# A click-model kernel on one Trainium2 core: the dense head after the history loop, laid out anew

## The chip, the core and the metric

The kernel runs on one core of a Trainium2 chip. That core has a matrix engine (TensorE, PE in the profile), VectorE (DVE), ScalarE (ACT), GpSimd (POOL) and SyncE (SP), each with an instruction queue of its own that runs in order; they meet through semaphores. On-chip data lies in SBUF (128 rows, or partitions) and in PSUM, into which PE writes its sums. DMA queues move data to and from the device's memory. The metric is the device time of one execution in microseconds (us).

## What is computed

The reference is a recommendation model with attention over a user's history. There are B = 16384 samples, each with L = 200 items of history; every table row has D = 64 numbers. Everything is float32.

```python
def dice(x, alpha, axis):
    mean, var = mean and variance of x along axis
    p = sigmoid((x - mean) * rsqrt(var + EPS))
    return x * (p + alpha * (1.0 - p))
u, it, c = u_emb[user], i_emb[item], c_emb[cate]      # B x 64 each
h = i_emb[hist]                                       # L x B x 64
feat = concatenate([h, it, h - it, h * it])           # L x B x 256
a = dice(feat @ au_W1 + au_b1, au_alpha, axis=1)      # L x B x 36
w = a @ au_W2 + au_b2                                 # L x B x 1
cur = sum(w * h, axis=0)                              # B x 64
z = concatenate([u, it, c, cur])                      # B x 256
z = dice(z @ W1 + b1, alpha1, axis=0)                 # B x 80
z = dice(z @ W2 + b2, alpha2, axis=0)                 # B x 40
return z @ W3 + b3                                    # B x 2
```

Two things matter for the order of the work. A dice needs the mean and the variance over the whole batch, so that each of its layers has to be finished before the next can start. And of the four inputs of the head's first layer only `cur` needs the loop over the history: `u`, `it` and `c` are there from the beginning.

## The kernel before

**Tiling.** The 16384 samples are 128 partitions by NT = 128 row tiles. Eight chunks (ND = 8) of TD = 16 row tiles each cover the batch; a chunk is 2048 samples. Transposed, with the 64 numbers of a row along the partitions, a chunk has CD = 1024 columns, with samples of one half of the row tiles on one half of the partitions (this is the `g` of the code: two groups of samples share 128 partitions). A step of the main loop is one chunk of one history position, so there are 200 x 8 = 1600 steps.

**Prologue (L194-270).** The item table is copied to device memory as `table`, each row followed by its product with a part of the first attention weight, so that one gather brings both. `fetch_one` and `keep_one` gather the rows of item, user and category (384 gathers, L138), transpose them and keep the item's in `itT`, and put the others into device memory as `ucT`. `xi`, the item's share of the attention layer, goes there too.

**Main loop.** `For_i` at L411 runs 8 times over 24 history positions each (192 steps); the last 8 positions (64 steps) are straight-line code (L415), with ten more steps that only drain. The order within a step is written out by hand, in `step` (L376), and is kept on each engine:

- `fetch(k)`: 16 indirect DMAs on POOL (L138) bring 128 rows each into one of 12 `land` buffers; SP loads `xit` (L309).
- ACT: a sigmoid into `gate` (L386) and a scaling into the PSUM buffer `pg` (L389), for step k-10.
- ACT: copy `xit` into PSUM buffer `px` (L391), two buffers taken in turn.
- `turn(k-1)`: four transposes on DVE from `land` into `hx` (L317); ACT copies the result to PSUM, `ph` (L393).
- `hidden(k-2)`: DVE adds (L329) and takes statistics (L331).
- `product(k-1)`: DVE multiplies into `hm` (L323), PE adds `hm` times a weight onto `px` (L176).
- After every eighth step, `moments` (L357-374) turns the statistics into the factors of dice, for one history position.
- `weigh(k-10)`: DVE forms the weight of each row from `pg` through `yT` and adds the weighted rows onto `cur` (L337 to L353).

A gather may write a `land` buffer only when `weigh` has done with it. Before the first step, ten `land` buffers and both `hx` are zeroed on DVE (L286, L288).

**Head (L418-507).** It stands behind the loop. Its weights are loaded there by SP (L429 to L444). Layer 1 takes each chunk c and each group g by itself: four inputs (user from `ucT`, item from `itT`, category from `ucT`, `cur` transposed by four DVE transposes) times `w1[g]`, whose rows for the other group are zero, into 80 partitions of `px[g]`. `keep` (L455) copies them with the bias to SBUF as `z` (ACT, L457) and takes statistics (DVE, L459). `col_moments` (L472) forms the factors of dice; `dice` (L477) is a sigmoid on ACT (L480) and a tensor_scalar on DVE (L481), with a product at L487; layer 2 goes from 80 to 40 partitions, again 16 times. Then dice again (product at L500), and layer 3: 256 matmuls of two columns each (L503), which give the result with samples along the partitions, an addition of the bias (L504), and one DMA (L507).

Of the kernel before, what the change touches and what calls it, by code (L numbers as in the profile page):

```python
# [14 lines left out]
P = 128  # L15
# [13 lines left out]
def din_kernel(  # L29
# [53 lines left out]
    blk_h = const.tile([P, P], F32, name="blk_h")  # L83
    blk_i = const.tile([P, P], F32, name="blk_i")
    blk_m = const.tile([P, P], F32, name="blk_m")
    au_w = const.tile([P, 4, A], F32, name="au_w")
# [39 lines left out]
    px = [psum.tile([P, CD], F32, name=f"px{i}") for i in range(2)]  # L126
# [6 lines left out]
    ucT = dram.tile([2, ND, P, CD], F32, name="ucT")  # L133

# [59 lines left out]
    with ExitStack() as start:  # L194
        pre = start.enter_context(tc.tile_pool(name="pre", bufs=3))
        ids = [start.enter_context(tc.tile_pool(name=f"ids{i}", bufs=1)).tile(
            [P, NT], I32, name=f"ids{i}") for i in range(3)]
        for t, v in zip(ids, (r_item, r_user, r_cate)):
            load_ids(t, v)
        load_hist_ids(0, 0)  # L200

        per = V // P
        rest = V - P * per
        grid = i_emb[: P * per].rearrange("(p n) d -> p n d", n=per)
        grid_out = table[: P * per].rearrange("(p n) d -> p n d", n=per)
        blocks = [(n0, min(TD, per - n0)) for n0 in range(0, per, TD)]
        if blocks[-1][1] == TD and rest:
            blocks.append((per, 0))
        tabs = {}

        def table_rows(b):

            n0, n = blocks[b]
            tab = pre.tile([P, TD, 2 * D], F32, tag="tab", name="tab")
            m = n
            if n:
                nc.sync.dma_start(tab[:, :n, :D], grid[:, n0 : n0 + n])
            if b == len(blocks) - 1 and rest:
                nc.vector.memset(tab[:, n, :D], 0.0)
                nc.sync.dma_start(tab[:rest, n, :D], i_emb[P * per :])  # L220
                m = n + 1
            rT = pre.tile([P, CD], F32, tag="rT", name="rT")
            transpose(rT, tab, m)
            layer(px[b % 2], [(blk_h, rT)], n=m * S)
            tabs[b] = tab, m

        def table_store(b):
            n0, n = blocks[b]
            tab, m = tabs.pop(b)
            transpose_back(tab[:, :, D:], px[b % 2], m)  # L230
            if n:
                nc.scalar.dma_start(grid_out[:, n0 : n0 + n], tab[:, :n])
            if m > n:
                nc.scalar.dma_start(table[P * per :], tab[:rest, n])

        def fetch_one(j):
            c, k = j % ND, j // ND
            gather(land[j % EARLY][:, :, :D], ids[k][:, ts(c, TD)], (i_emb, u_emb, c_emb)[k])

        def keep_one(j):  # L240
            c, k = j % ND, j // ND
            if k == 0:
                transpose(itT[:, c], land[j % EARLY])
                layer(ph, [(blk_i, itT[:, c])])
                t = pre.tile([P, CD], F32, tag="t", name="t")
                nc.scalar.activation(t, ph, AF.Identity, bias=au_bias)
                nc.scalar.dma_start(xi[c], t)
            else:
                t = pre.tile([P, CD], F32, tag="t", name="t")
                transpose(t, land[j % EARLY])  # L250
                nc.scalar.dma_start(ucT[k - 1, c], t)

        with tc.manual_schedule():
            done = 0
            for j in range(3 * ND + 1):
                if j < 3 * ND:
                    fetch_one(j)
                while done < len(blocks) + 1 and done < 2 * j + 2 + j // 12:
                    if done < len(blocks):
                        table_rows(done)  # L260
                    if done:
                        table_store(done - 1)
                    done += 1
                if j:
                    keep_one(j - 1)
            while done < len(blocks) + 1:
                if done < len(blocks):
                    table_rows(done)
                table_store(done - 1)
                done += 1  # L270

    with ExitStack() as main:
# [7 lines left out]
        hm = ring.tile([P, CD], F32, name="hm")  # L280
        gate = ring.tile([P, CD], F32, name="gate")
        yT = ring.tile([P, CD], F32, name="yT")
# [7 lines left out]
        for t in px:  # L290
            layer(t, [(blk_m, hx[0][:, 0])])
# [29 lines left out]
        def product(k):  # L321

            nc.vector.tensor_mul(hm, ph, itT[:, k % ND])  # L323
            layer(px[k % 2], [(blk_m, hm)], onto=True)

        def hidden(k):

            l, c = divmod(k, ND)
            nc.vector.tensor_add(x_of(k), by_row(px[k % 2]), by_row(hx[k % 2][:, 1]))  # L329
            for i in range(2):  # L330
                nc.vector.bn_stats(  # L331
                    stats[l % 2][:, 2 * c + i, :], x_of(k)[:, ts(i, TD // 2)]
                )

        def weigh(k):

            nc.vector.tensor_mul(by_row(pg), by_row(pg), x_of(k))  # L337
            nc.vector.transpose(yT, pg)  # L338
# [37 lines left out]
        def step(k, last=None):  # L376
# [7 lines left out]
            if has(k - 10):  # L384
                i = (k - 10) // ND % 2
                nc.scalar.activation(  # L386
                    by_row(gate), x_of(k - 10), AF.Sigmoid, bias=shifts[i], scale=rstds[i]
                )
                nc.scalar.activation(pg, gate, AF.Identity, bias=au_al, scale=au_1al)  # L389
            if has(k - 1):  # L390
                nc.scalar.copy(px[(k - 1) % 2], xit[(k - 1) % XI])  # L391
                turn(k - 1)
                nc.scalar.copy(ph, hx[(k - 1) % 2][:, 0])  # L393
            if has(k - 2):
                hidden(k - 2)
            if has(k - 1):
                product(k - 1)
# [5 lines left out]
        def steps(l0, n, last):  # L403

            for k in range(n * ND + (10 if last else 0)):
                l, c = divmod(k, ND)
                if c == 0 and l + 1 < n + (not last):
                    load_hist_ids((l + 1) % IDX, l0 + l + 1)
                step(k, last=n * ND - 1 if last else None)

        with tc.For_i(0, L - L % LPB, LPB) as l0:  # L411
            with tc.manual_schedule():
                steps(l0, LPB, False)
        with tc.manual_schedule():
            steps(L - L % LPB, L % LPB, True)  # L415


    with ExitStack() as head:  # L418
        fin = head.enter_context(tc.tile_pool(name="fin", bufs=1))
        work = head.enter_context(tc.tile_pool(name="work2", bufs=2))  # L420


        w1 = []
        for g in range(2):
            t = fin.tile([P, 4, Z1], F32, name=f"w1{g}")
            nc.vector.memset(t, 0.0)
            for e in range(2):
                rows = W1.rearrange("(f d) z -> d f z", d=D)[e * S : (e + 1) * S]
                nc.sync.dma_start(t[quarter(e, g)], rows)  # L429
            w1.append(t)  # L430
        w2 = fin.tile([Z1, Z2], F32, name="w2")
        nc.sync.dma_start(w2, W2)
        w3 = fin.tile([Z2, ZO], F32, name="w3")
        nc.sync.dma_start(w3, W3)
        bias1 = fin.tile([Z1, 1], F32, name="bias1")
        nc.sync.dma_start(bias1, col(b1))
        bias2 = fin.tile([Z2, 1], F32, name="bias2")
        nc.sync.dma_start(bias2, col(b2))
        bias3 = fin.tile([P, ZO], F32, name="bias3")
        nc.sync.dma_start(bias3, b3.partition_broadcast(P))  # L440
        al, al1 = [], []
        for i, (v, n) in enumerate(((alpha1, Z1), (alpha2, Z2))):
            t = fin.tile([n, 1], F32, name=f"al{i}")
            nc.sync.dma_start(t, col(v))  # L444
            u = fin.tile([n, 1], F32, name=f"al1{i}")
            nc.vector.tensor_scalar(u, t, -1.0, 1.0, ALU.mult, ALU.add)
            al.append(t)
            al1.append(u)

        z = fin.tile([Z1, 2 * ND, CD], F32, name="z")  # L450
        zstats = [
            fin.tile([n, 4 * ND, nc.vector.BN_STATS_DIM], F32, name=f"stats{i}")
            for i, n in enumerate((Z1, Z2))
        ]
        def keep(i, n, m, pz, bias):  # L455

            nc.scalar.activation(z[:n, m, :], pz[:n], AF.Identity, bias=bias)  # L457
            for j in range(2):
                nc.vector.bn_stats(zstats[i][:, 2 * m + j, :], z[:n, m, ts(j, CH)])  # L459

        for c in range(ND):
            rows = land[c % EARLY].rearrange("p (s n) d -> p s (n d)", s=2)
            for i in range(2):
                nc.sync.dma_start(rows[:, i], ucT[i, c])
# [73 lines left out]
```

## Time and profile before

| | us |
|---|---|
| median of 3 runs (32900.82 to 32961.82) | 32900.87 |
| the profiled execution | 32903.59 |
| its span in the trace | 32901.7 |
| busy in the span: DVE | 25564.2 |
| busy in the span: POOL | 24520.4 |
| busy in the span: ACT | 7641.4 |
| busy in the span: PE | 6388.8 |

The span is what lies between the first and the last instruction that the trace shows; 1.9 us of the execution lie outside it. The mean clock that TensorE was granted is 0.546 of full speed. Of the busy time, 0.944 us is one gather's time on POOL; the DMA that it starts goes on by itself. The share of busy time is a mean over the whole kernel, and nearly all of the span is the main loop; a stage of some tens of us cannot be read from it and has to be read from the timeline and from busy times over a stretch.

How the rows are read: a row of a group gives line, engine, operation, the tile written and the tiles read, shapes and a count; then busy us and the mean ns of one, then the idle us of that engine just before such instructions, with what ended most of it ("issue": nothing that the trace shows). A row of the timeline gives start, duration, engine and instruction, and in brackets the idle time before it. "x2" in a row of the PE counts passes: a float32 matmul is recorded as two. `128*80` in such a row is the stationary operand, 128 rows by 80 columns.

### The profile page before, as it was taken

To read this page: it belongs to the slowest core of one execution; us is meant where nothing else is said; L and a number is where in the kernel's file an instruction comes from. 1 tells how busy PE (TensorE), PEld (TensorE's weight loads), DVE (VectorE), ACT (ScalarE), POOL (GpSimd) and SP (SyncE) were. 2 spreads that over 40 slices of the span, in tenths; PEclk is the share of its full clock that TensorE was granted. 3 is DMA by queue.
4 is the path that set the end of the run, shared out by engine and by line. 5 is a ranking of instruction groups with operands and counts; after the bars stand their busy time and mean duration, and the time that the engine had idled before them with its cause. 6 is when DMAs were issued, how large, how long until landed. Compare 5 with 4: busy or idle time off the path is not lost. (4 is left out here: it accounts for less than half of the span.)

```text
span 32901.7 us, 99907 instructions
## 1 busy us (share of the span) xinstructions
PE 6388.8 (19%) x7216; PEld 2043.0 (6%) x7216; DVE 25564.2 (78%) x28837; ACT 7641.4 (23%) x7113; POOL 24520.4 (75%) x25988
## 2 busy tenths in 40 slices
PE   3111111111111111111111111111111111111113
PEld 0000000000000000000000000000000000000001
DVE  7777777777777777777777777777777777777776
ACT  1222222222222222222222222222222222222222
POOL 7777777777777777777777777777777777777774
PEclk6555555555555555555555555555555555555555
DMA  5222222222222222222222222222222222222221
GB/s 158 79 79 79 79 79 79 79 80 78 80 79 79 79 78 80 79 79 80 78 79 79 80 79 79 80 79 79 79 79 80 79 80 78 79 80 79 80 79 53
DMA packets 1208006, 2648.96 MB, mean 81 GB/s; under 512 B 549078, under 2 KB 575222, under 8 KB 1201142
## 3 DMA queue, kind: packets, MB, share of 16 engines
q0 software_dynamic: 831488, 1691.97, 19.8%
q1 hardware_dynamic: 365238, 887.18, 8.5%
q10 hardware_dynamic: 10560, 63.79, 0.5%
q14 instruction: 705, 5.78, 0.1%
q8 instruction: 15, 0.25, 0.0%
HBM read 2577.24 MB, written 63.91 MB: 80 GB/s over the span
## 5 line engine op out<-in xcount | busy, mean ns | idle before, releaser
L138 POOL DMA_INDIRECT land<-table,idx x25600 | 24157.7, 944 | 7880.7 <-issue 7560.7
L317 DVE STREAM_TRANSPOSE hx<-land 64x1024 f32<-64x1024 f32 x6404 | 7935.6, 1239 | 6418.2 <-DMA land<-table,idx 6265.7
L176 PE MATMUL px<-hm,blk_m 128*128 128x512 f32 x6404 | 5973.2, 1088 | 26045.0 <-DVE hm L323 26045.0
L389 ACT ACTIVATE pg<-gate,au_al,au_1al 128x1024 f32<-128x1024 f32 x1610 | 1943.8, 1207 | 12855.1 <-DVE cur L353 12854.8
L393 ACT COPY ph<-hx 128x1024 f32<-128x1024 f32 x1601 | 1627.7, 1017 | 10702.8 <-DVE hx L317 10702.8
L176 PEld LDWEIGHTS px<-hm,blk_m 128*128 128x128 f32 x6404 | 1878.9, 324 | 30138.6 <-DVE hm L323 28484.2
L331 DVE BATCH_NORM_STATS2 st<-land 128x6 f32<-128x512 f32 x3204 | 2060.6, 685 | 55.0
L338 DVE STREAM_TRANSPOSE yT<-pg 128x1024 f32<-128x1024 f32 x1610 | 2011.6, 1249 | 55.2
L352 DVE TENSOR_TENSOR pg<-land,ph 128x1024 f32<-128x1024 f32 x1610 | 1978.6, 1229 | 54.9
L353 DVE TENSOR_TENSOR cur<-pg,cur 128x1024 f32<-128x1024 f32 x1610 | 1971.2, 1224 | 55.6
L340 DVE TENSOR_REDUCE r<-yT 128x32 f32<-128x1024 f32 x1610 | 1964.0, 1220 | 55.3
L329 DVE TENSOR_TENSOR land<-px,hx 128x1024 f32<-128x1024 f32 x1602 | 1961.2, 1224 | 49.4
L386 ACT ACTIVATE gate<-land,sh,rs 128x1024 f32<-128x1024 f32 x1610 | 1991.7, 1237 | 2.9
L337 DVE TENSOR_TENSOR pg<-pg,land 128x1024 f32<-128x1024 f32 x1610 | 1967.5, 1222 | 10.7 <-ACT pg L389 10.7
L323 DVE TENSOR_TENSOR hm<-ph,itT 128x1024 f32<-128x1024 f32 x1601 | 1931.1, 1206 | 0.0
L391 ACT COPY px<-xit 128x1024 f32<-128x1024 f32 x1601 | 1591.4, 994 | 22.9 <-PE px L176 22.9
L347 DVE SCALAR_TENSOR_TENSOR ph<-r,au_bias,r 64x16 f32<-64x16 f32 x3220 | 770.7, 239 | 114.7
L386 ACT ACT_TABLE_LOAD x210 | 269.4, 1283 | 582.1 <-DMA land<-table,idx 372.3
L344 DVE COPY r<-r 64x32 f32<-64x32 f32 x1610 | 321.4, 200 | 55.0
L185 ACT ACT_TABLE_LOAD x203 | 260.4, 1283 | 3.6
L185 ACT ACTIVATE std<-var,eps 128x1 f32<-128x1 f32 x201 | 59.2, 295 | 716.5 <-DVE var L373 716.5
L176 PE MATMUL px<-rT,blk_h 128*128 128x512 f32 (+1 forms) x196 | 158.2, 942 | 231.1 <-DVE rT L159 231.1
(76 smaller groups left out, 1903.2 us busy)
## 6 DMA issues: line engine op xcount, KB each, us to landing
xit<-xi SPq DMA_DIRECT2D x1601, 512.0 KB, 3.9
land<-table,idx POOLq DMA_INDIRECT x25600, 2.5
table<-tab ACTq DMA_DIRECT2D x48, 1024.0 KB, 4.4
tab<-in_L_rec_i_emb SPq DMA_DIRECT2D x48, 512.0 KB, 4.3
idx<-in_r_hist SPq DMA_DIRECT2D x200, 64.0 KB, 1.8
ucT<-t ACTq DMA_DIRECT2D x16, 512.0 KB, 2.9
land<-ucT SPq DMA_DIRECT2D x16, 512.0 KB, 4.3
xi<-t ACTq DMA_DIRECT2D x8, 512.0 KB, 2.7
```

The source lines that it names most:

```text
L138: nc.gpsimd.indirect_dma_start(out=dst[:, n, :], out_offset=None, in_=rows, in_offset=bass.IndirectOffsetOnAxis(ap=ids[:, n : n + 1], axis=0),
L176: nc.tensor.matmul(dst[:, cols], lhsT, rhs[:, cols], start=(j == 0 and not onto), stop=(j == len(pairs) - 1), skip_group_check=onto,)
L317: nc.vector.transpose(dst.rearrange("p s (n t) -> p n s t", t=S), rows[ts(i, D), :, :, e])
L329: nc.vector.tensor_add(x_of(k), by_row(px[k % 2]), by_row(hx[k % 2][:, 1]))
L331: nc.vector.bn_stats(stats[l % 2][:, 2 * c + i, :], x_of(k)[:, ts(i, TD // 2)])
L337: nc.vector.tensor_mul(by_row(pg), by_row(pg), x_of(k))
L338: nc.vector.transpose(yT, pg)
L340: nc.vector.tensor_reduce(r, yT.rearrange("p (i n u) -> p i n u", i=2, u=S), mybir.AxisListType.X, ALU.add)
L352: nc.vector.tensor_mul(by_row(pg), rows, w.unsqueeze(2).to_broadcast([P, TD, D]))
L353: nc.vector.tensor_add(cur[:, ts(c, TD)], by_row(pg), cur[:, ts(c, TD)])
L386: nc.scalar.activation(by_row(gate), x_of(k - 10), AF.Sigmoid, bias=shifts[i], scale=rstds[i])
L389: nc.scalar.activation(pg, gate, AF.Identity, bias=au_al, scale=au_1al)
```

## The change

**Placement.** The pools `pre` and `once` are opened early and closed before the loop; the weights that only the prologue needs move to `once`. The head's tiles are allocated at the start. The two buffers `px[0]`, `px[1]` become `px`, used by every step, and `pz`. `hm` and `yT` become parts of `hx`, and `gate` becomes `pg` in place: the sigmoid and the scaling both write `pg`.

```diff
+    px, pz = (psum.tile([P, CD], F32, name=n) for n in ("px", "pz"))
...
-                    by_row(gate), x_of(k - 10), AF.Sigmoid, bias=shifts[i], scale=rstds[i]
+                    by_row(pg), x_of(k - 10), AF.Sigmoid, bias=shifts[i], scale=rstds[i]
...
-                nc.scalar.activation(pg, gate, AF.Identity, bias=au_al, scale=au_1al)
+                nc.scalar.activation(pg, pg, AF.Identity, bias=au_al, scale=au_1al)
...
-                nc.scalar.copy(px[(k - 1) % 2], xit[(k - 1) % XI])
                 turn(k - 1)
                 nc.scalar.copy(ph, hx[(k - 1) % 2][:, 0])
...
                 hidden(k - 2)
...
+                nc.scalar.copy(px, xit[(k - 1) % XI])
                 product(k - 1)
```

**Packing.** The 80 units of layer 1 are split into 64 (ZA) and 16 (ZB). The 64 of both groups of samples fill 128 partitions, one tile for each chunk. The 16 of both groups are 32 partitions, and four chunks (J = 4) share one tile of 128, each in a window of its own of a weight that is zero elsewhere. Layer 2's 40 units of both groups are 80 partitions; layer 3's two outputs of both groups and all eight chunks are 32 partitions, again by windows. A unit then has its statistics on several partitions; the mean over these is taken by a small matmul with a matrix `mean_of`, built at the very start from a unit matrix:

```diff
+    for n, t in mean_of.items():
+        m = t.shape[0] // n
+        unit = once.tile([n, m, n], F32, name=f"unit{n}")
+        nc.vector.memset(unit, 0.0)
+        nc.gpsimd.affine_select(
+            out=unit, in_=unit, compare_op=ALU.not_equal, fill=1.0, base=0,
+            pattern=[[0, m], [-1, n]], channel_multiplier=1,
+        )
+        unit = unit.rearrange("u m v -> u (m v)")
+        nc.tensor.matmul(ph[: n * m, : n * m], unit, unit, start=True, stop=True)
+        nc.vector.tensor_scalar_mul(t, ph[: n * m, : n * m], 1.0 / m)
```

In the built program the two first gathers of the prologue stand ahead of the three affine selects on POOL, and an instruction that loads GpSimd's library stands between them; it is not in the kernel before.

**Weights.** They are loaded at the end of the prologue, before the zeroing of `land`: five memsets on DVE (512, 896, 80, 320 and 60 columns), some 45 small DMAs on SP, three tensor_scalars.

```diff
+    def load_head_weights():
+        for t in (w1a, w1b, w2a, w2b, w3):
+            nc.vector.memset(t, 0.0)
+        for g in range(2):
+            for e in range(2):
+                rows = W1.rearrange("(f d) z -> d f z", d=D)[e * S : (e + 1) * S]
+                nc.sync.dma_start(w1a[quarter(e, g), :, ts(g, ZA)], rows[:, :, :ZA])
+                z0 = 2 * ZB * (J - 1) + ZB * g
+                nc.sync.dma_start(w1b[quarter(e, g), :, z0 : z0 + ZB], rows[:, :, ZA:])
...
```

**Loop.** The For_i runs 7 times; the last 32 positions (256 steps) are straight-line code. In these, `base_of_layer1` sums item, user and category for layer 1, one matmul of 512 columns behind each step (96 of them, and a step or two at each of ten evictions, in which the sum with its bias goes to device memory as `zbase`).

```diff
+                    for f, t in ((1, itT[:, c]), (0, zt[:, 0]), (2, zt[:, 1])):
+                        w = w1b[:, f, window(j)] if rest else w1a[:, f]
+                        for i in range(2):
+                            nc.tensor.matmul(
+                                pz[:, ts(i, CH)], w, t[:, ts(i, CH)],
+                                start=(f == 1 and j == 0), stop=(f == 2 and last),
+                            )
+                            yield
+                    if last:
+                        nc.scalar.activation(
+                            zt[:, 0], pz, AF.Identity, bias=(zb if rest else za)[0]
+                        )
+                        nc.sync.dma_start(zbase[ND + c // J if rest else c], zt[:, 0])
```

**Drain and head.** In the ten draining steps the fourth input is added, a chunk behind each of the last eight weighings. SP loads `zbase` into free `land` buffers, ACT copies it to PSUM, DVE transposes `cur`, and PE adds:

```diff
+            load_base(0, 1)
+            for k in range(K, K + 10):
+                step(k, last=K - 1)
+                if k < K + 4:
+                    load_base(*((2, 3), (ND, ND + 1), (4, 5), (6, 7))[k - K])
+                c = k - K - 2
+                if c >= 1:
+                    keep1(c - 1)
+                if c >= 0:
+                    layer1(c)
+            keep1(ND - 1)
...
+        def layer1(c):
+            nc.scalar.copy(px, z_of(c))
+            if c % J == 0:
+                nc.scalar.copy(pz, rest_of(c))
+            curT = xit[c % XI]
+            transpose(curT, cur[:, ts(c, TD)])
+            layer(px, [(w1a[:, 3], curT)], onto=True)
+            layer(pz, [(w1b[:, 3, window(c % J)], curT)], onto=True)
+        def keep1(c):
+            nc.scalar.copy(z_of(c), px)
+            row_sums(0, P, c, z_of(c))
+            if c % J == J - 1:
+                nc.scalar.copy(rest_of(c), pz)
+                row_sums(1, P, c // J, rest_of(c))
```

Layers 2 and 3 then go over eight chunks instead of sixteen; layer 3's matmuls all add onto one tile of 32 partitions, which is transposed once at the end:

```diff
+            fa, fb = row_factors(0, ZA, P), row_factors(1, ZB, P)
+            for c in range(ND):
+                if c % J == 0:
+                    dice(rest_of(c), rest_of(c), spare[4 + c // J], fb, zb)
+                a = spare[c % 4]
+                dice(a, z_of(c), a, fa, za)
+                po = (px, pz, pg, ph)[c % 4]
+                layer(po[: 2 * Z2], [(w2a, a), (w2b[:, c % J], rest_of(c))])
+                t = home(10 + c)[: 2 * Z2]
+                nc.scalar.activation(t, po[: 2 * Z2], AF.Identity, bias=z2[0])
+                row_sums(2, 2 * Z2, c, t)
+            f2 = row_factors(2, Z2, 2 * Z2)
+            for c in range(ND):
+                a = spare[c % 4]
+                dice(a, home(10 + c)[: 2 * Z2], a, f2, z2)
+                at = (ND - 1 - c) * 2 * ZO
+                for i in range(2):
+                    nc.tensor.matmul(
+                        px[:n, ts(i, CH)], w3[:, at : at + n], a[: 2 * Z2, ts(i, CH)],
+                        start=(c == 0), stop=(c == ND - 1),
+                    )
...
```

`row_sums` is two bn_stats on DVE, `row_factors` a bn_aggr, two matmuls of one column with `mean_of`, a few small DVE operations and the square root on ACT; `dice` is, as before, a sigmoid on ACT, and a tensor_scalar and a product on DVE.

## The prediction, made before the changed kernel ran

> **What bounds the kernel now.** First the groups of instructions, for who waits for whom (count | busy us, mean ns | idle us before them and its releaser).
>
> ```profile
> L138 POOL DMA_INDIRECT land<-table,idx x25600 | 24157.7, 944 | 7880.7 <-issue 7560.7
> L317 DVE STREAM_TRANSPOSE hx<-land 64x1024 f32<-64x1024 f32 x6404 | 7935.6, 1239 | 6418.2 <-DMA land<-table,idx 6265.7
> L389 ACT ACTIVATE pg<-gate,au_al,au_1al 128x1024 f32<-128x1024 f32 x1610 | 1943.8, 1207 | 12855.1 <-DVE cur L353 12854.8
> ```
>
> POOL issues a gather in 0.944 us, then idles for nothing but issue. DVE waits 6418.2/1601 = 4.0 us a step for a gather to land. So gathers set the pace: 16 x 1.249 = 19.98 us a step (1.249: start to start in the timeline), and any other engine has 4.0 us to spare. Second, the timeline of POOL, for what breaks its row:
>
> ```profile
> 536.33 0.94 POOL L138 DMA_INDIRECT land<-table,idx  x1 [7.25 <-issue]
> ...
> 27411.51 0.94 POOL L138 DMA_INDIRECT land<-table,idx  x1 [10.69 <-issue]
> ...
> 32526.55 0.95 POOL L138 DMA_INDIRECT land<-table,idx  x1 [0.30 <-issue]
> ```
>
> Only nine gaps exceed 0.45 us: one at the main loop's start, seven at loop boundaries (a middle one costs 10.69 - 0.30 = 10.4), one at its exit. The last gather is issued at 32527.5; all after it is on the path. Third, that end in stretches (us; busy PE, PEld, DVE, ACT, POOL with counts; PE clock; DMA share; GB/s): drain, layer 1, layer 2, layer 3.
>
> ```profile
> 32527.50:32625.50 98.00, 4.30 (x5) 1.51 (x6) 82.02 (x107) 25.84 (x22) 0.00 (x0) 0.50 0.11 35
> 32625.50:32739.00 113.50, 111.05 (x256) 38.42 (x254) 43.06 (x65) 19.04 (x17) 0.00 (x0) 0.99 0.15 47
> 32739.00:32811.00 72.00, 56.35 (x64) 10.62 (x64) 51.66 (x68) 39.29 (x35) 0.00 (x0) 0.51 0.00 0
> 32811.00:32901.70 90.70, 55.88 (x256) 55.19 (x256) 33.34 (x44) 21.32 (x18) 0.00 (x0) 0.50 0.01 2
> ```
>
> 98.0 + 113.5 + 72.0 + 90.7 = 374.2 us. PE is the wall in layer 1 (111.05 of 113.5). Last, the chain of waits, for the clock and the size of the runs:
>
> ```profile
> 32624.99 111.58 PE px L176 x256
> ...
> 32745.63 10.45 PE px L176 x12
> ...
> 32819.06 7.00 PE ph L503 x32
> ```
>
> A pass costs 111.05/256 = 0.434 us in layer 1 (clock 0.99), and 10.45/12 = 0.87 in layer 2 (clock 0.51).
>
> **The change, part by part (after-kernel's lines named "new").**
>
> *Before the last gather.* (a) The unit matrices put a GpSimd library load and three affine selects (new L167) into POOL's row, behind two gathers. No row shows either. Below: POOL's nearest row, a memset, takes 0.1 us, so 0.5 in all, and no less since nothing is removed. Above: the Trainium skill, "GPSIMD Engine Reference", section 2.1 Instruction dispatch, gives about 6 us for the first call after code is loaded. I take 6 + 3 x 0.5 and some issue = 8 (an estimate from that page, as the memset needs no code load), ends 0.5 and 20. The products of these matrices on PE and DVE (new L172, L173) wait for the selects, with the table's first blocks behind them; DVE has 342.8 of 470 us to do in the prologue, and takes that delay in its idle 127. (b) The head's weights are loaded between prologue and loop. DVE's five memsets there and three tensor_scalars stand ahead of the first weighing, for which POOL's row stops (the 7.25): by the 128x2048 memset's 1.76 per 2048 columns, 1868 columns make 1.7, with 5 x 0.38 issue and 0.8 for the small ones = 4.4, all on the path; bounds 0 and 10. Their 45 odd DMAs cost SP about 0.4 each (SPq L429: 0.42), 19 us, beside nine to eleven memsets of 2.14 each; without that cover SP's first xit loads would be late by the rest, which is the 10. (c) Seven iterations in place of eight: -10.4. The longer straight-line part brings no gaps by the row: the 64 steps that ran so before have none. Sum: 8 + 4.4 - 10.4 = **+2.0**.
>
> *In the steps.* The sigmoid writes pg, so it waits for the preceding cur (L353): 1.24 + 1.21 = 2.45 us, needed only after the 4.0 wait, the turn (5.0), hidden (2.5) and product (1.2). Queued behind it on ACT is the ph copy, itself waiting for the turn. The px copy goes behind hidden; it ends 1.2 + 1.0 = 2.2 after the turn, hm ends 3.7 after it. Both hidden; each has over 1.5 us left. Some 116 steps of the last 256 carry one more matmul (2 passes, 1.7; PE has 16 of 20 us idle), now and then an eviction (1.1 on ACT, 80% idle), and 16 loads and 10 stores of 512 KB on SP. POOL passes none of it: its pitch was 1.249 too in the prologue, at 214 GB/s. **0**, and if the cover of 4.0 went, each us over would cost 1 us a step.
>
> *Drain with layer 1 (new L571-582).* Up to the end of step K+1 as before: 29.7 (L353 of step K+5 starts at 32589.56; four drain steps of 8.39 back and 1.23 on, 32557.2). Then eight weighings at 7.05 (L337 at 32592.12 to the end of L353) = 56.4. Step K+2 waits for sigmoid and affine, 2.5 (before: 1.34 in each; later the transposes cover it). Eight times four transposes: 8 x 2.88 = 23.0. Statistics: seven pairs in the steps, two of the packed rest: 9 x 1.28 = 11.5 (the tenth lies under PE). PE's eight passes a chunk lie beside the next weighing except the last: cold 6.9, then a copy 1.0. SP's ten loads of 512 KB from zbase land in 3.9, a step ahead of their use. Sum **131.0**, in place of 98.0 + 113.5: the fourth input's PE work is hidden and only DVE's share remains.
>
> *Factors.* Two chains (bn_aggr 1.0 and 0.6, two tiny matmuls each, sqrt 0.3, small DVE operations) with a table load 1.28 and the first sigmoid 1.24: **8.1**; before layer 3 again: **6.2** (before: 32737.73 to 32743.42 = 5.7 with statistics, but without matmuls).
>
> *Layer 2.* Eight chunks instead of sixteen half-used ones, but serial: the next tensor_scalar stands on DVE behind the statistics of this chunk. Each: 0.80 + 1.22 + PE + 1.11 + 1.28 + 0.3 waits. PE runs 8 passes of 128*80. Here a rule speaks against the change. Rows: in layer 1,
>
> ```profile
> 32624.98 1.97 PE L176 MATMUL px<-land,w 128*80 128x512 f32 x2 [83.25 <-DMA w<-in_L_rec_W]
> 32628.24 1.02 PE L176 MATMUL px<-land,w 128*80 128x512 f32 x2
> ```
>
> 128*80 passes were at full speed 3.3 us after their start; but the 80*40 run of 10.45 us never was. The Trainium skill, "TensorE: Matmul & The Clock Gate", section "HAM oscillation", warns of PE gaps over about 3.4 us: each puts the clock back to half. The gaps here are about 4.7 us, where layer 1 ran 111 us unbroken. By the rule each chunk starts cold, warms after some 3.4 us: 4 x 0.87 + 4 x 0.434 = 5.2. By the 80*40 row: 8 x 0.87 = 7.0. The form 128*80 is the nearer row; I take 5.6, as the phase of the warm-up is free, ends 3.5 and 7.0. So 8 x 10.3 + two dices of the packed rest, 2 x 2.05 = **86.5**; ends 70 and 98.
>
> *Layer 3.* 256 small matmuls go; 32 passes of 80*32 come, accumulating in px. First dice 2.05. The nearest row is 80*40, which stayed cold: 32 x 0.87 = 27.8, above DVE's 8 x 2.05. By the rule it would warm and DVE would set 17. I take **27.8**, ends 17 and 28. Then one transpose 1.3, four additions 1.7, output 2.9 (from 32898.83 to 32901.7 before) = 5.9 + 2.05 = **8.0**.
>
> Sum: 131.0 + 8.1 + 86.5 + 6.2 + 27.8 + 8.0 = **267.6** against 374.2: -106.6. With +2.0: **-104.6**. The profiled execution took 32903.6 us (span 32901.7 and 1.9 around it), so 32799 like it; it lay 2.7 over the median of the runs, 32900.87, from which I forecast **32796**. What can be told from no change is 0.2%, 66 us.
>
> **Rivals.**
> 1. *PE warm through layers 2 and 3* (chance 0.17): 8 x 2.1 + 11 less: about 32768. For it: full clock in layer 1. Against: clock 0.51 over all of layer 2.
> 2. *All cold* (0.17): + 8 x 1.4, and waits between ACT and PE in the drain that the sum leaves out, 5: about 32812. With more such waits, up to 25 more (0.05).
> 3. *The code load is dear* (0.07): if it and the selects take 50 us or more, little of the gain is seen: 32840 to 32900. Against: nothing but a page's 6 us; POOL's row has no such thing.
> 4. *Slower* (0.04): place: POOL's every gather after the code load. If what is loaded leaves the gather's own code slower, each of about 25,980 pays. From 104.6/25,980 = 4.0 ns on 944 all is lost; at 1% (9.4 ns) it is +245: about 33,040. For it: gathers are POOL's own work and its sole bound. Against: 944 is the same over both tables.
>
> The forecast itself has 0.50. Range 32752 to 32838: from rival 1 with a cheap code load to rival 2 with its extra waits. Faster by over 0.2%: 0.50 + 0.17 + 0.17 + 0.05 = 0.89; within: 0.07; slower: 0.04.
>
> **What would show it.** Gathers stay at 944 and 1.249; DVE's wait before L317's successor stays near 4 us; between the second and third gather a gap of about 8; one boundary fewer; the gap near 529 is about 4.4 longer. After the last gather 268 us, with PE's 128*80 groups near 5.6 per chunk and 80*32 at 0.87 a pass. I am wrong if gathers lengthen, if PE waits or ACT waits hold the weighing in the drain (steps over 11.2), or if the clock is otherwise in layer 2.

## The result, and the profile after

The changed kernel takes **32784.95 us** (median of 7 runs, 32783.09 to 32786.09) where the kernel before takes 32900.87: a ratio of 0.9964, 95% interval 0.9955 to 0.9973. That is 115.9 us less. The forecast was 32796 and 104.6 less. The profiled execution took 32783.09 us, with a span of 32780.9.

The groups of instructions, in the columns of before (count | busy us, mean ns | idle before, releaser):

```profile
L202 POOL DMA_INDIRECT land<-table,idx x25600 | 24152.2, 943 | 7872.6 <-issue 7703.8
L377 DVE STREAM_TRANSPOSE hx<-land 64x1024 f32<-64x1024 f32 x6404 | 7938.2, 1240 | 6360.3 <-DMA land<-table,idx 6218.5
L448 ACT ACTIVATE pg<-land,sh,rs 128x1024 f32<-128x1024 f32 x1610 | 1943.8, 1207 | 12980.0 <-DVE cur L415 11593.3
L451 ACT ACTIVATE pg<-pg,au_al,au_1al 128x1024 f32<-128x1024 f32 x1610 | 1895.0, 1177 | 54.3
```

The gathers still set the pace: the row of POOL is as before, and DVE still waits 6360.3/1601 = 4.0 us a step for rows to land. What was added to the steps is not seen here. The 12.9 ms for which ACT stood before its scaling now stand before the sigmoid (L448, 13.0 ms), one instruction earlier, and cost as little.

The timeline of POOL where its row is broken (start, duration, instruction, idle before it):

```profile
11.22 0.95 POOL L202 DMA_INDIRECT land<-in_L_rec_i_emb,ids  x1 [0.30 <-issue]
12.60 0.79 POOL L167 TENSOR_SCALAR_AFFINE_SELECT unit<-unit 64x128 f32<-64x128 f32 x3 [0.42 <-DVE unit L166]
13.61 0.95 POOL L202 DMA_INDIRECT land<-in_L_rec_i_emb,ids  x1 [0.23 <-issue]
...
539.53 0.94 POOL L202 DMA_INDIRECT land<-table,idx  x1 [9.45 <-issue]
...
23565.08 0.94 POOL L202 DMA_INDIRECT land<-table,idx  x1 [10.69 <-issue]
...
27402.62 0.94 POOL L202 DMA_INDIRECT land<-table,idx  x1 [3.36 <-issue]
...
32514.03 0.94 POOL L202 DMA_INDIRECT land<-table,idx  x1 [0.30 <-issue]
```

The three selects take 0.79 us together, and no time of a code load is to be seen: the third gather starts 13.61 - 11.22 = 2.39 us after the second instead of 1.25, so 1.1 us is what they cost. The gap at the start of the main loop has grown from 7.25 to 9.45. The first gather behind the loop starts at 27402.6 instead of 31249.4, after six boundaries instead of seven. The last gather ends at 32515.0; before it was 32527.5.

All that follows is the end, in stretches (us; busy PE, PEld, DVE, ACT, POOL with counts; PE clock; DMA share; GB/s): drain with layer 1, factors, layer 2, factors, layer 3.

```profile
32514.97:32643.69 128.72, 50.92 (x68) 19.21 (x68) 115.24 (x156) 47.70 (x45) 0.00 (x0) 0.66 0.08 29
32643.69:32651.04 7.35, 1.91 (x8) 1.60 (x8) 2.05 (x11) 3.08 (x5) 0.00 (x0) 0.66 0.00 0
32651.04:32738.78 87.74, 47.33 (x64) 13.87 (x64) 29.77 (x36) 19.02 (x17) 0.00 (x0) 0.68 0.00 0
32738.78:32745.27 6.49, 0.58 (x4) 0.43 (x4) 1.26 (x5) 4.09 (x5) 0.00 (x0) 0.72 0.00 0
32745.27:32780.90 35.63, 27.52 (x32) 5.49 (x32) 18.56 (x21) 8.33 (x7) 0.00 (x0) 0.50 0.02 4
```

The end takes 265.9 us instead of 374.2. DVE is busy in 115.24 of the first 128.72 us: layer 1 is now DVE's transposes and statistics, and PE's part of it is hidden. Layer 2 has become longer, 87.7 for 72.0, with PE busy for just over half of it: it has 64 passes as before (eight chunks of eight instead of sixteen halves of four), but PE now waits 40 us for its inputs. Layer 3 is 35.6 for 90.7.

The kernel before did not wait in this way. In its timeline DVE forms the input of the second of the sixteen (L481 at 32745.41) before the statistics of the first one's output (L459):

```profile
32743.42 0.81 DVE L481 TENSOR_SCALAR p<-p,al,al 80x1024 f32<-80x1024 f32 x1 [2.65 <-ACT p L480]
...
32745.41 0.80 DVE L481 TENSOR_SCALAR p<-p,al,al 80x1024 f32<-80x1024 f32 x1
...
32750.70 1.27 DVE L459 BATCH_NORM_STATS2 stats<-z 40x6 f32<-40x512 f32 x2
```

In the changed kernel the order of the code puts each chunk's statistics ahead of the next chunk's input.

The chain of waits, for the PE runs:

```profile
32665.57 5.86 PE pz L240 x8
...
32698.32 6.53 PE px L240 x8
...
32747.39 27.53 PE px L604 x32
```

Eight passes of layer 2 take 5.4 to 6.5 us, neither all at full clock (3.5) nor all at half (7.0); layer 3's 32 passes take 0.86 each at clock 0.50.

Eight of the twelve experiments below ran on three other chips than the first four, and there all kernels are slow: 36730 to 36898 us, and 36940 to 37007 for the kernel before beside them. DVE stands idle there between short instructions of the loop (last section). From these runs layers 2 and 3 are compared, where single instructions last as long as in the changed kernel's profile; the stretch from the last gather to layer 2 is some 18 us longer there in every kernel.

### The profile page after: what moved, and what is told of

The parts are those of the page before. It is cut to its first block, busy times and chain, and to the rows that moved or that the text cites. A ratio compares the mean times of both kernels' runs of the same rounds, so it can differ in the third digit from the quotient of the medians.

```text
span 32780.9 us, 100656 instructions
## 1 busy us (share of the span) xinstructions
PE 6366.6 (19%) x7006; PEld 2038.0 (6%) x7006; DVE 25567.4 (78%) x28797; ACT 7755.2 (24%) x7105; POOL 24515.6 (75%) x25991
## 5 line engine op out<-in xcount | busy, mean ns | idle before, releaser
L377 DVE STREAM_TRANSPOSE hx<-land 64x1024 f32<-64x1024 f32 x6404 | 7938.2, 1240 | 6360.3 <-DMA land<-table,idx 6218.5
L240 PE MATMUL px<-hx,blk_m 128*128 128x512 f32 x6408 | 5927.6, 1080 | 26007.0 <-DVE hx L384 25941.1
L448 ACT ACTIVATE pg<-land,sh,rs 128x1024 f32<-128x1024 f32 x1610 | 1943.8, 1207 | 12980.0 <-DVE cur L415 11593.3
L240 PEld LDWEIGHTS px<-hx,blk_m 128*128 128x128 f32 x6408 | 1880.1, 324 | 30022.8 <-issue 29846.4
L400 DVE STREAM_TRANSPOSE hx<-pg 128x1024 f32<-128x1024 f32 x1610 | 2011.7, 1250 | 55.2
L402 DVE TENSOR_REDUCE r<-hx 128x32 f32<-128x1024 f32 x1610 | 1964.0, 1220 | 55.3
L384 DVE TENSOR_TENSOR hx<-ph,itT 128x1024 f32<-128x1024 f32 x1601 | 1932.0, 1207 | 0.0
L451 ACT ACTIVATE pg<-pg,au_al,au_1al 128x1024 f32<-128x1024 f32 x1610 | 1895.0, 1177 | 54.3
L425 DVE COPY other<-mv 32x2 f32<-32x2 f32 x804 | 155.6, 194 | 15.1
```

Of the source, the lines that this page charges most:

```text
L240: nc.tensor.matmul(dst[:, cols], lhsT, rhs[:, cols], start=(j == 0 and not onto), stop=(j == len(pairs) - 1), skip_group_check=onto,)
L377: nc.vector.transpose(dst.rearrange("p s (n t) -> p n s t", t=S), rows[ts(i, D), :, :, e])
L402: nc.vector.tensor_reduce(r, yT.rearrange("p (i n u) -> p i n u", i=2, u=S), mybir.AxisListType.X, ALU.add)
L448: nc.scalar.activation(by_row(pg), x_of(k - 10), AF.Sigmoid, bias=shifts[i], scale=rstds[i])
```

## The experiments

### Ahead of the last gather

**Without the affine selects.**

```diff
-        nc.vector.memset(unit, 0.0)
-        nc.gpsimd.affine_select(
-            out=unit, in_=unit, compare_op=ALU.not_equal, fill=1.0, base=0,
-            pattern=[[0, m], [-1, n]], channel_multiplier=1,
-        )
+        nc.vector.memset(unit, 1.0 / n)
```

> The changed kernel without the three affine selects and so without the GpSimd library load; the unit matrices are filled with a constant instead, so that the mean over partitions is left out. Theory (the selects cost POOL only the 1.15 us by which its third gather starts later): third gather at about 12.5 us instead of 13.61, last gather about 1.1 earlier or less, pitch 1.2482 as in the changed kernel. Rival (the loaded library is what shortens a gather from 943.65 to 943.43 ns on average): the mean gather is back at 943.65 ns, the last gather ends about 5.7 - 1.1 = 4.6 us later than in the changed kernel.

The timeline of POOL in this kernel, at its first gathers:

```profile
11.45 0.95 POOL L198 DMA_INDIRECT land<-in_L_rec_i_emb,ids  x1 [0.30 <-issue]
12.70 0.94 POOL L198 DMA_INDIRECT land<-in_L_rec_i_emb,ids  x1 [0.30 <-issue]
```

The third gather follows the second by 1.25 again: 1.1 us is the whole price of the selects and of what is loaded for them. The rival falls: a gather's mean over all is 943.51 ns here, without the library, and 943.45 in the changed kernel. The time, 32784.6, cannot tell a difference of 1 us.

**The loop's split alone, in the kernel before.**

```diff
-        with tc.For_i(0, L - L % LPB, LPB) as l0:
+        rest_l = L % LPB + LPB
+        with tc.For_i(0, L - rest_l, LPB) as l0:
...
-            steps(L - L % LPB, L % LPB, True)
+            steps(L - rest_l, rest_l, True)
```

> The kernel before with only the loop's split changed: 7 iterations of 24 positions and 32 straight-line ones instead of 8 and 8. Theory: one boundary of 10.4 us less, so the last gather ends at 32527.5 - 10.4 = 32517.1 and the time is about 32890.5. Rival (the longer straight-line part pays for its code elsewhere, or the pitch of 1.2484 changes with it): last gather not between 32514 and 32520.

The time was 32893.3 (one run; the kernel before beside it 32906.9, and 32900.9 in the other runs), so 7.5 to 13.6 less. The idle times over 0.45 us in POOL's row add up to 71.4 us against 81.9: 10.5 less, one boundary. From the first gather's start to the last one's end it is 32505.8 us against 32517.6, 11.8 less; what is over 10.5 is the mean gather again (943.56 ns here, 943.66 in the profile before). The longer straight-line part costs nothing.

**Without the summing of the three inputs during the loop.**

```diff
-            work = base_of_layer1()
+            work = iter(())
...
-                nc.sync.dma_start(z_of(c), zbase[c])
+                nc.sync.dma_start(z_of(c), ucT[c // ND, c % ND])
```

> The changed kernel without the summing of user, item and category during the last 256 steps (96 matmuls, 10 evictions, 32 loads and 10 stores left out; the drain loads other data of the same size). Theory (all of it lies beside the gathers, which set the pace): time within 3 us of the changed kernel, 32782 to 32788, and the same pitch of gathers in the last 2048 gathers (1.2482). Rival (the extra DMAs or the ACT evictions delay the steps a little): faster by more than 3 us.

32784.3 us, against 32784.95 with it. In the last 1024 gathers the pitch is 1.2482 us here and 1.2483 in the changed kernel. The 192 passes, ten evictions and 42 transfers (32 loads and 10 stores) are free where they stand.

**The head's weights in the middle of the prologue.**

```diff
+            if j == 12:
+                load_head_weights()
...
-        load_head_weights()
```

> The changed kernel with the head's weights loaded in the middle of the prologue instead of between prologue and loop. Theory (the 9.45 us gap of POOL at 530 is longer than the 7.25 before because DVE's first weighing is late by the memsets and tensor_scalars): the gap falls to 7.3, the last gather ends about 2.1 us earlier. Rival (the gap grew for SP's queue, whose loads of xit and idx stand behind the weights, or DVE's prologue becomes late and the first table gather waits): the gap stays at 9.4, or another one opens before it.

The timeline of POOL at the main loop's start:

```profile
537.62 0.94 POOL L202 DMA_INDIRECT land<-table,idx  x1 [7.31 <-issue]
```

The gap is 7.31, so 2.1 us of it came from where the weights were loaded. The move takes away DVE's memsets and SP's loads together; that it was DVE follows from the changed kernel's timeline, where DVE works from 494.8 to the first weighing at 533.0 with no gap over 0.38 us. The time did not fall (32788.3 us, one run), and the last gather did not end earlier: from the first gather it is 32509.4 us, 4.2 more than in the changed kernel, because the mean gather was 943.75 ns instead of 943.45. This scatter from run to run (943.45 to 943.75 over these four profiles and those before and after, 8 us in 25,984 gathers) is larger than this part's price. DVE stood 18.3 us in the middle of the prologue for the weights, which delayed no gather here.

### Behind the last gather

**Layer 3 with 128 columns.**

```diff
-    w3 = const.tile([2 * Z2, (2 * ND - 1) * 2 * ZO], F32, name="w3")
+    w3 = const.tile([2 * Z2, (ND - 1) * 2 * ZO + P], F32, name="w3")
...
-                        px[:n, ts(i, CH)], w3[:, at : at + n], a[: 2 * Z2, ts(i, CH)],
+                        px[:, ts(i, CH)], w3[:, at : at + P], a[: 2 * Z2, ts(i, CH)],
```

> The changed kernel with layer 3's weight tile read 128 columns wide instead of 32 (the columns behind are zeros, the rows of px behind the 32 are not read). The count of passes and of streamed columns stays. Theory (the clock follows how much of the array a pass uses: 128*80 in layer 2 warms, 80*32 and 80*40 never do): the clock rises after some 3.3 us and the 32 passes fall from 27.5 us to what DVE supplies, 8 x 2.05 = 16.4 to 18; time 9 to 11 us less, about 32775. Rival (the clock does not follow the width but the run's start, its gaps or its operand rows): 27.5 us at clock 0.50 again, same time.

A miss (36762.7 us; the kernel before on that chip 36940.4). The timeline, and the stretch of layer 3's passes in the columns above:

```profile
36725.97 27.68 PE L603 MATMUL px<-land,w 80*128 80x512 f32 x32 [6.78 <-DVE land L565]
```
```profile
36725.90:36753.70 27.80, 27.68 (x32) 10.61 (x32) 13.90 (x16) 6.28 (x6) 0.00 (x0) 0.50 0.00 0
```

Four times as many columns, and the clock stays at 0.50. The passes stand back to back for 27.7 us, so gaps are not the reason either. Nor is it the chip: in the same run layer 2, with 128 rows, has a clock of 0.68 as in the changed kernel. What is left of the form is its 80 rows.

**Layer 3 with 128 rows, and with 128 rows and columns.**

```diff
-    w3 = const.tile([2 * Z2, (2 * ND - 1) * 2 * ZO], F32, name="w3")
+    w3 = const.tile([P, (ND - 1) * 2 * ZO + ND * 2 * ZO], F32, name="w3")
...
-                        px[:n, ts(i, CH)], w3[:, at : at + n], a[: 2 * Z2, ts(i, CH)],
+                        px[:n, ts(i, CH)], w3[:, at : at + n], a[:, ts(i, CH)],
```

> The changed kernel with layer 3 fed with 128 rows instead of 80 (the weight's rows 80 to 127 are zero, the data's are left over from layer 2), 32 columns as before; the count of passes stays. Theory (what keeps the clock low in layer 3 is that a pass uses 80 of 128 operand rows; the width was shown not to matter at 80 rows): the clock rises after some 3.5 us and the 32 passes fall from 27.5 us to 16 to 18, bounded by DVE. Rival (rows and columns must both be large, or the clock has another cause in this stage): 27.5 us at clock 0.50.

> As the run with 128 rows, and 128 columns too. If rows alone decide: the same 16 to 18 us as with 32 columns. If the used share of the array (rows by columns) decides: 27.5 us with 32 columns and 16 to 18 us here. If neither: 27.5 us in both.

The groups of instructions of the first kernel in its last 55 us, and the stretch of these passes:

```profile
L604 PE MATMUL px<-land,w 128*32 128x512 f32 x32 | 16.1, 669 | 6.8 <-DVE land L565 6.8
```
```profile
36819.10:36835.30 16.20, 16.14 (x32) 3.81 (x32) 13.59 (x15) 6.22 (x6) 0.00 (x0) 0.86 0.00 0
```

With 128 rows the same 32 passes take 16.1 us at a mean clock of 0.86: five start 0.85 us apart, the sixth is in between, and the rest follow at 0.43. With 128 columns too it is 16.2. So the rows decide and the columns don't. The added 48 rows are zeros in the weight; they add nothing to the result and save 11.4 us. Their data is what layer 2 left there, so whether the clock follows the rows in use or the numbers that move in them is not separated. The times are 36844.5 and 36898.0 us (the kernel before on that chip 36987.1); their difference lies ahead of the last gather.

**Layer 2 with the dice one chunk ahead.**

```diff
+            feed(0)
             for c in range(ND):
-                if c % J == 0:
-                    dice(rest_of(c), rest_of(c), spare[4 + c // J], fb, zb)
-                a = spare[c % 4]
-                dice(a, z_of(c), a, fa, za)
                 po = (px, pz, pg, ph)[c % 4]
-                layer(po[: 2 * Z2], [(w2a, a), (w2b[:, c % J], rest_of(c))])
+                layer(po[: 2 * Z2], [(w2a, spare[c % 4]), (w2b[:, c % J], rest_of(c))])
+                if c + 1 < ND:
+                    feed(c + 1)
                 t = home(10 + c)[: 2 * Z2]
```

`feed(c)` holds the lines taken out.

> The changed kernel with the dice of chunk c+1 put ahead of the eviction and statistics of chunk c in layer 2, so that PE can run without the gap of 4.5 us between chunks. Theory ([...]each chunk pays four cold passes): PE runs at full clock after the first 3.5 us, 8 chunks of 3.5 to 3.7; layer 2 takes about 4.1 + 8 x 3.6 + 1.7 + 2.4 = 37 us instead of 87.7, time about 32734. Rival 1 (the clock stays low in this stage anyway): 8 x 7.0 + 6.5 = 62, time about 32759. Rival 2 (the serial part is not the order but the buffers or ACT): 75 or more.

First the passes of the changed kernel's first chunk and the starts of its second and third, in its timeline; then three chunks of this kernel in the chain of waits, the fifth of them in its timeline, and its whole layer 2 as a stretch:

```profile
32655.15 1.99 PE L240 MATMUL px<-land,w2a 128*80 128x512 f32 x2 [7.00 <-DVE land L565]
32656.94 1.91 PE L240 MATMUL px<-land,w2b 128*80 128x512 f32 x2
32658.64 1.58 PE L240 MATMUL px<-land,w2a 128*80 128x512 f32 x2
32660.06 1.02 PE L240 MATMUL px<-land,w2b 128*80 128x512 f32 x2
...
32665.57 1.99 PE L240 MATMUL pz<-land,w2a 128*80 128x512 f32 x2 [4.49 <-DVE land L565]
...
32675.90 1.12 PE L240 MATMUL pg<-land,w2a 128*80 128x512 f32 x2 [4.49 <-DVE land L565]
32676.83 1.90 PE L240 MATMUL pg<-land,w2b 128*80 128x512 f32 x2
```
```profile
36656.29 3.67 PE pg L240 x8
...
36666.52 5.33 PE px L240 x8
36671.85 3.45 PE pz L240 x8
```
```profile
36666.52 1.06 PE L240 MATMUL px<-land,w2a 128*80 128x512 f32 x2 [3.11 <-DVE land L565]
36667.41 1.63 PE L240 MATMUL px<-land,w2b 128*80 128x512 f32 x2
36668.83 1.91 PE L240 MATMUL px<-land,w2a 128*80 128x512 f32 x2
```
```profile
36641.60:36685.96 44.36, 32.45 (x64) 10.19 (x64) 29.70 (x36) 19.02 (x17) 0.00 (x0) 0.86 0.00 0
```

In the changed kernel seven of the eight chunks start cold, that is at half clock (two passes in 1.99 us), and are warm, at full clock, after some 4 us; PE then waits about 4.5 us. The third still starts warm (1.12) and turns cold after its second pass. Without these waits six of the chunks take 3.45 to 3.67 us, and layer 2 takes 44.4 us instead of 87.7 (87.5 in the run with 128 columns, on the same chip; this run's time was 36730.3 us, that one's 36762.7). Of the 43.4 us, the warm clock is 14.9 (PE busy 32.45 instead of 47.33); the other 28.5 are waits of PE that the order takes away. The expected 37 was too low mostly for the fifth chunk: the dice of the second packed rest comes in between, PE waits 3.1 us, its passes turn cold after the second, and they take 5.33.

**Combined, and with a longer loop body.** The three edits together (layer 3 with 128 rows and columns, layer 2 one chunk ahead, weights early), and then also:

```diff
-LPB = 24
+LPB = 48
```

Each has two results, since gathers did not set the pace the first time.

> The changed kernel with layer 2's dice one chunk ahead, the head's weights loaded in the prologue, and layer 3 with 128 rows and 128 columns. Theory: layer 2 takes 44 us instead of 87.7 (as the run of that part alone), the gap at 530 us 7.3 instead of 9.45, layer 3's passes 17 instead of 27.5 if the clock rises: 32785 - 43.5 - 2.1 - 10 = 32729; without the clock's rise 32739. Rival (the parts disturb each other, or the first passes of layer 2 were warm by chance): over 32745.

> As the combined kernel, with 48 positions in the loop's body: 3 iterations and 56 straight-line positions instead of 7 and 32. Theory (each boundary costs 10.4 us of POOL, as the run that took one away showed): 4 boundaries less, 41.6 us less than the combined kernel. Rival (a longer body pays more for its code, at each boundary or between): less than 35 us gained, with larger gaps in POOL's row.

> The combined kernel once more (layer 2 one chunk ahead, weights in the prologue, layer 3 with 128 rows and columns)[...]. Where gathers set the pace (pitch 1.248 with few gaps): 267 - 44 - 11.5 = 212 us after the last gather, time 32785 - 43.5 - 2.1 - 11.5 = 32728. Where DVE's instructions come late again: about 0.9964 of the kernel before, as then.

> The same with 48 positions in the loop's body. Where gathers set the pace: 4 boundaries of 10.4 us less than the combined kernel, 32728 - 41.6 = 32686. Rival (a longer body pays for its code): less than 35 us gained. Where DVE's instructions come late again: about 35 us less than the combined kernel, as then.

| | combined | longer body | kernel before beside them |
|---|---|---|---|
| first time, us | 36856.1 | 36821.7 | 36987.1 |
| ratio to before (95%) | 0.9963 (0.9949 to 0.9977) | 0.9953 (0.9937 to 0.9970) | |
| second time, us | 36876.5 | 36829.2 | 37007.0 |
| ratio to before (95%) | 0.9965 (0.9952 to 0.9977) | 0.9951 (0.9935 to 0.9968) | |

Gathers did not set the pace either time, so the numbers expected for a loop paced by them were not tested. Behind the last gather the combined kernel takes 228.7 and 228.5 us in its two profiles. The run with 128 rows and columns, which has the same layer 3 and ran on the same chip as the first, takes 272.5: 43.8 less, which is layer 2's 43.4. The run that changes only layer 3's width, whose layer 3 took as long as the changed kernel's, takes 284.9 on another chip: 56 less, the 43.4 of layer 2 and the 11.4 of layer 3 within 2 us.

What lies ahead of the last gather did not keep that. From first to last gather it is 36464.7 us in the kernel with 128 columns, and on the other chip 36557.9 with 128 rows, 36612.7 with 128 rows and columns, and 36619.4 in the first combined one, though their loop is the same code; the combined kernel's 36856.1 us are no less than the 36844.5 of layer 3 with 128 rows alone. Part of it is the third edit. In all four profiles with the weights in the prologue, DVE waits 35 to 36 us there for their loads and POOL stands 37.5 to 38.9 us for DVE; the prologue's gathers take 604 to 612 us, against 575 to 584 in the four slow profiles without that edit. So here the edit that was to save 2 us costs some 20 to 37. The rest of the 155 us between the extremes lies in the loop and stays open; the kernel before, too, differs by 47 us between these two chips.

So it is shown that the end gets 56 us shorter; that the combined kernel beats the changed one where gathers set the pace is only to be expected. The longer body is 34.4 and 47.4 us faster than the combined kernel by the medians (31 and 34 in the profiles' loops). The first lies below the 35 that the rival named, so the 41.6 is not confirmed.

## Why the prediction was right

The mechanism and most sizes held; the step that was off most lies ahead of the last gather. The time came out 11 us under the forecast, 6.9 of them from that step.

| term of the sum | predicted | measured |
|---|---|---|
| library load and selects (a) | +8 | +1.1 |
| weights ahead of the first weighing (b) | +4.4 | +2.2 |
| one boundary less (c) | -10.4 | -10.2 |
| drain with layer 1 | 131.0 | 128.7 |
| factors | 8.1 | 7.4 |
| layer 2 | 86.5 | 87.7 |
| factors | 6.2 | 6.5 |
| layer 3, with the output | 35.8 | 35.6 |
| sum behind the last gather | 267.6 | 265.9 |

The end as a whole: 374.2 - 265.9 = 108.3 of the 115.9 us, predicted 106.6. Terms (a) to (c) sum to -6.9 instead of +2.0 (a boundary's 10.4 went, and the loop's exit costs 0.2 more: 3.36 for 3.13); with -108.3 that is -115.2, and the medians differ by 115.9.

- **(a) was the mis-sized term.** The prediction took the 6 us that the Trainium skill ("GPSIMD Engine Reference", section 2.1 Instruction dispatch) gives for the first call after a load, over the nearest row of the trace, a memset of 0.1 us. The trace shows 0.42 of waiting for DVE's memset and 0.79 for three selects, and without them 1.1 us less. The row was the better guide, and the page's 6 us are not seen here. Rival 3 (a dear load) and rival 4 (gathers that slow down after it) fall with the same runs: gathers are 943.45 ns with it and 943.51 without.
- **(b)** was right in place, as moving the load took 2.1 of the gap away, at half the price. The five small memsets follow each other within 0.2 us, and the tensor_scalars directly, without the 0.38 us of issue that the 2048-column memsets show.
- **The steps** were rightly put at 0: the run without the summing takes the same time, and DVE's wait of 4.0 us a step has not changed. The summing has 32 loads, not the 16 of the prediction, since each input is read for both tiles; they cost nothing either.
- **The drain** is bound by DVE as predicted: in the last steps 11.06 us each (12.25 with the packed rest's statistics), against 7.05 + 2.88 + 1.28 = 11.2.
- **Layer 2** took 5.9 us of PE a chunk (47.33/8), predicted 5.6, since between four and six passes are cold where four were assumed. The rule that speaks against the change (the Trainium skill, "TensorE: Matmul & The Clock Gate", section "HAM oscillation": gaps over about 3.4 us put the clock back) describes this stage in the main: the gaps were 4.5, and closing them brought the clock from 0.68 to 0.86. It is not exact here: a gap of 3.1 us (the fifth chunk of that run) put the clock back too, two passes after it, and gaps of 1.1 us did not. The prediction took the row of the same form (128*80) over the row of the same layer (80*40); that was right, and layer 3's runs show why: it is the rows.
- **Layer 3** stayed cold as its nearest row had said, where the rule (the Trainium skill, the same page, section "What's actually happening") would have had it warm after about 3.4 us of unbroken work. The trace's row held and the rule did not: 27.5 us with 80 rows did not warm it.
- **Rival 1** (warm through both layers) did not come, but it is what the runs one chunk ahead and with 128 rows bring about. Their passes take 14.9 + 11.4 = 26 us less, close to the 28 that it was given; the other 28.5 us that they save are waits. **Rival 2** (all cold) was wrong in layer 2 by 7.0 - 5.9 = 1.1 us a chunk.

One thing the profiles show has no cause in the change: from first to last gather the changed kernel's profile is 12.5 us shorter, of which the gaps explain 6.9. The other 5.5 are a mean over all 25,984 gathers of 943.45 instead of 943.66 ns. The six profiles of kernels with and without parts of the change, in loops that gathers pace, lie between 943.45 and 943.75 with no order in it, so it is taken for scatter; the profiled execution before was also 2.7 us above its median, and that after 1.9 below.

## What to carry to other kernels

A tail behind a loop that is paced by one engine is worth as much as its whole length: sum what does not depend on the loop inside it, where the idle engines do it for nothing, and pack what is left into all 128 partitions. Packing does not take away waits: layer 2, with 64 passes before and after, became longer (87.7 for 72.0 us) because its order by hand put each chunk's output ahead of the next chunk's input on an in-order engine, and was shorter (44.4) once that order was turned round. Where the trace has a form of the same rows, take its time per pass over a rule.

## What was not expected of the hardware

In these runs the granted clock followed the operand's rows. Passes with 80 rows stayed at half clock through 27.5 us without a break (80 by 32 and 80 by 128 columns), and passes with 128 rows, of which 48 are multiplied by zeros, reached full clock with 32 columns just as with 128. In the mean over the 32 a pass took 0.86 us with 80 rows and 0.50 with 128, warm-up included. It was tried for layer 3 alone, not for row counts in between.

On three chips DVE stood between short instructions with nothing that the trace shows to wait for. The timeline of DVE in the kernel with 128 columns, within a `moments`:

```profile
20027.65 0.16 DVE L425 COPY other<-mv 32x2 f32<-32x2 f32 x1 [3.66 <-issue]
20028.36 0.38 DVE L425 COPY other<-mv 32x2 f32<-32x2 f32 x1 [0.55 <-issue]
20029.75 0.24 DVE L425 COPY other<-mv 32x2 f32<-32x2 f32 x1 [1.01 <-issue]
```

The starts are 0.7 and 1.4 us apart for work of 0.2 to 0.4. Over the whole kernel DVE stood 1140 us before these 804 copies, against 15 in the changed kernel's profile. A step of the loop then took 22.4 to 22.5 us instead of 19.98. DVE in place of POOL set the pace: its waits for rows to land, 6218.5 us in the changed kernel, are down to 46.9. The kernel before was as slow (36940 to 37007 us). That the code arrived late is a guess; no run here shows it.
